# Gathered graph messages with a layer norm: the ramp-down of a software pipeline over the last groups is spread from 12 groups to 36, and the last node block is written out

## The chip, the cores and the metric

The kernel runs on one core of a Trainium2 chip. The metric is the device time of one execution in microseconds (us), as a median over runs. A core has a matrix engine (TensorE, PE in the profile), a vector engine (VectorE, DVE), a scalar engine (ScalarE, ACT), GpSimd (POOL), a queue engine (SyncE, SP) that here only issues transfers, and 16 DMA engines that they share.

## The reference, cut to what matters

There are 12,500 nodes with 64 features (`x`) and 200,000 edges, sorted by their target `dst`; `src` is random. Targets are drawn as 12,500·u² with u uniform, so low nodes have most edges; towards the end of the list a group of 512 edges moves on by some 64 nodes.

```python
def ssp(x): return softplus(x) - log(2.0)
nodes = x[stack([src, dst], 1)].reshape(E, 128)              # gather both ends of each edge
gates = (ssp(edge_state @ We1 + be1) @ We2 + be2) * (1 - sigmoid(5 * (edges_distance - 3.5)))
h = ssp(nodes @ Wn1 + bn1) @ Wn2 + bn2
message_sum = zeros_like(x).at[dst].add(h * gates)           # scatter-add into the targets
new_state = x + (ssp(message_sum @ Ws1 + bs1) @ Ws2 + bs2)   # a small network on every node
out = layernorm(x + new_state)                               # over the 64 features, no scale or shift
```

## The kernel before, in words

The edges are cut into NG = 391 groups of 512, numbered 0 to 390 (`last`). The last group is partly padding: it has three gathers, not four. A group goes through these operations, each a small function:

- `gather` (L176): GpSimd issues four indirect transfers of 128 rows of `x` each into `xg`. In every 32nd group, the last of them 388, the fourth set of rows comes by single-row transfers on SyncE (L191) in place of the fourth gather. `load` brings edge features (`eT`, L197) and a 42-row window of a prepared table (`wns`, L204) on SyncE.
- `onehot` (L209, VectorE) writes a one-hot code of each edge's target within the window beside the gathered rows.
- `transposes` (L217, four on TensorE) into the PSUM tile `tx`, `xcopy` (L222, ScalarE) out of it.
- `layer1`: edge part (L226 bias, L228), node part (L233, four matmuls), into the PSUM tile `z`.
- `exps` and `logs` (L243, L246, ScalarE), then `softplus` (L251, VectorE).
- `layer2`: bias and edge part (L257, L260), node part (L265, eight matmuls), into `gh`.
- `hcut` and `message` (L270, L274, VectorE).
- `scatter` (L278, four matmuls) sums messages into the window, and `window` (L287, two adds on VectorE at an offset read from a table) adds the result into `sums`, the running message sum of all nodes in SBUF.

The main loop has steps i. Every engine runs its instructions in the order in which the loop writes them; waits between engines are put in by the framework from what is read and written, and an add at an offset known only at run time counts as touching all of `sums`. The pipeline is staggered: step i transposes group i+3, does layer 1 of group i+1, layer 2 of i-1 and the scatter of i-3. There are two `tx` buffers, which the transposes, the late scatters and the node blocks share, two of `z` and two of `gh`.

At step `both` = `last` - CATCH_UP = 378 this stagger is reduced at one go: two groups get layer 2 in that step, three are scattered in the next, and from then on step i transposes i+2, does layer 1 of i+1, layer 2 of i and the scatter of i-1 (into `tx`, no longer into a corner of `z`). The last group is written into the last steps by hand, its softplus in an edge and a node part.

The nodes are cut into blocks of 512 (the first has 212, the last two 256). `block_steps` gives the number of groups after which a block's sums are surely complete; towards the end 359, 368, 376, 384, 388 and 391. `node_block` then queues five parts in `todo`, and a step takes one of them: `hidden` (L306, matmuls that read `sums`) with `clamp` (L312 loads `x`, L314 and L315 on VectorE); `logs` and `ssp` (L318, L319 ScalarE, L322 VectorE); `layer2` of the block (L327, L330) with `center` (L334 to L337: add, mean over features, subtract); `square` and `variance` (L341 ScalarE, L345 and L346 VectorE); `root` and `store` (L350, L351 ScalarE, L356 to L359 VectorE, and L360, the store on SyncE). Parts that are left after the loop run one behind the other.

Of the kernel before, what the change touches and what calls it, by code (L numbers as in the profile page):

```python
# [40 lines left out]
F32 = mybir.dt.float32  # L42
BF16 = mybir.dt.bfloat16
I32 = mybir.dt.int32
AF = mybir.ActivationFunctionType
# [19 lines left out]
CATCH_UP = 12  # L65
# [7 lines left out]
def node_blocks(N):  # L73

    rest = N - NB
    first = rest % NB
    assert rest > 0 and first % 2 == 0 and first <= HE
    sizes = ([first] if first else []) + [NB] * (rest // NB) + [HE, HE]
    return [(sum(sizes[:i]), n) for i, n in enumerate(sizes)]
# [18 lines left out]
def gnn_resnorm_kernel(ctx: ExitStack, tc: tile.TileContext, a: dict, out: bass.AP, E: int):  # L98
# [52 lines left out]
    half = const.tile([P, 1], F32, name="half")  # L151
    ones3 = const.tile([PIECES, HE], BF16, name="ones3")
# [78 lines left out]
    def layer1_node(g, h):  # L231
        zn = zs[g][:, h, HE * (1 - h) : HE * (2 - h)]
        nc.tensor.matmul(zn, wns[:, g % REST, h, :], xTs[g][:, h], start=True, stop=True, skip_group_check=True)  # L233
# [29 lines left out]
    def layer2_node(g, h):  # L263
        for t in range(2):
            nc.tensor.matmul(ghs[g][:, 1, 2 * t + h, :], ss[g][:, 1 + h, t, :], wn2, start=False,  # L265
                             stop=h == 1 and t == 1, skip_group_check=True)
# [14 lines left out]

    def window(g):
        for h in range(2):
            base = nc.values_load(base_i[0:1, 2 * g + h : 2 * g + h + 1], engines=[DVE], min_val=0, max_val=N - 1,
                                  skip_runtime_bounds_check_because="it was clamped to these bounds")
            part = sums[h * D : (h + 1) * D, bass.ds(base, W)]
            nc.vector.tensor_add(part, part, scs[g][h * D : (h + 1) * D, h * W : (h + 1) * W])  # L287

    def node_block(first, n, pool):
# [20 lines left out]
        def clamp():  # L310
            t["y"] = tile3("y")
            nc.sync.dma_start(t["y"], x[rows, :].rearrange("(q p k) d -> p q k d", q=nq, k=2))  # L312
            t["l"], t["zb"] = (pool.tile([P, HE], F32, name=name, bufs=2) for name in ("l_s", "zb"))
            nc.vector.tensor_scalar(t["l"], t["z"], packed["bs1"], BIG, OP.add, OP.min)  # L314
            nc.vector.tensor_scalar(t["zb"], t["z"], packed["bs1"], None, OP.add)  # L315
# [17 lines left out]
        def center():  # L333
            nc.vector.scalar_tensor_tensor(t["y"], t["y"], 2.0, t["u"][:, :nq], OP.mult, OP.add)  # L334
            mean = small("mean")
            nc.vector.tensor_reduce(mean, t["y"], AX.X, OP.add)
            nc.vector.scalar_tensor_tensor(t["y"], mean.to_broadcast([p, nq, 2, D]), -1.0 / D, t["y"], OP.mult, OP.add)  # L337
# [5 lines left out]
        def variance():  # L343
            t["v"] = small("var")
            nc.vector.tensor_reduce(t["v"], t["y2"], AX.X, OP.add)  # L345
            nc.vector.tensor_scalar(t["v"], t["v"], 1.0 / D, EPS, OP.mult, OP.add)  # L346

        def root():
            t["r"] = small("rstd")
            nc.scalar.activation(t["r"], t["v"], AF.Ln)  # L350
            nc.scalar.activation(t["r"], t["r"], AF.Exp, scale=-0.5)  # L351

        def store():

            v, r = t["v"], t["r"]
            nc.vector.tensor_mul(v, v, r)  # L356
            nc.vector.scalar_tensor_tensor(v, v, -0.5, r, OP.mult, OP.mult)
            nc.vector.scalar_tensor_tensor(r, v, 1.5, r, OP.add, OP.mult)
            nc.vector.tensor_mul(t["y"], t["y"], r.to_broadcast([p, nq, 2, D]))  # L359
            nc.sync.dma_start(out[rows, :].rearrange("(q p k) d -> p q k d", q=nq, k=2), t["y"])  # L360

        def then(f, g):
            def both():
# [4 lines left out]
        return [(hidden, clamp), (None, then(logs, ssp)), (layer2, center), (None, then(square, variance)),  # L368
                (None, then(root, store))]
# [6 lines left out]
    with tc.manual_schedule():  # L376
# [4 lines left out]
        with tc.tile_pool(name="prep", bufs=1) as prep:  # L381
# [23 lines left out]
            nc.vector.memset(half, 0.5)  # L405
            nc.vector.memset(ones3, 1.0)
# [40 lines left out]
            nc.vector.tensor_add(brow[:, 1:3, :], brow[:, 1:3, :], ps[:1, : 2 * D].rearrange("o (i d) -> o i d", d=D))  # L447
            pieces = prep.tile([1, PIECES, 4 * D], BF16, name="pieces")
# [43 lines left out]
        with tc.tile_pool(name="finish", bufs=1) as finish:  # L492
            blocks = list(zip(node_blocks(N), block_steps(N, NG)))
            last = NG - 1
            both = last - CATCH_UP
            second, third, ahead = {}, {}, {}
            for i in range(-3, NG + 1):
                groups = [i - 1] if i < both else [i - 1, i] if i == both else [i]
                second[i] = [g for g in groups if 0 <= g < NG]
                groups = [i - 3] if i <= both else [i - 3, i - 2, i - 1] if i == both + 1 else [i - 1]  # L500
                third[i] = [g for g in groups if g >= 0]
                groups = [i + 3] if i < both else [] if i == both else [i + 2]
                ahead[i] = [g for g in groups if g < NG]
            todo, complete = [], 0
# [9 lines left out]
            for i in range(-3, NG + 1):  # L514
                part = todo.pop(0) if todo else None
                at(load, i + LOADS)
                fetch(i)
                if i > 0:
                    at(gather, i + AHEAD - 1)
                if i < both:  # L520
                    if 0 <= i + 1:
                        zs[i + 1] = z_tile()
                    for g in third[i]:
                        scatter(g, zs[i + 1][:, 1, HE : HE + 2 * W])
                    for g in second[i]:
                        layer2_edge(g)
                elif i + 1 < last:
                    zs[i + 1] = z_tile()
                if i + 1 < last:
                    at(layer1_edge, i + 1)  # L530
                    at(layer1_node, i + 1, 0)
                    at(layer1_node, i + 1, 1)
                if part and part[0] and i + 2 < last:
                    part[0](tx_tile())
                for g in ahead[i]:
                    transposes(g)
                if i + 1 < last:
                    at(exps, i + 1)
                    if i < both:
                        at(logs, i + 1)  # L540
                for g in ahead[i]:
                    xcopy(g)
                if i >= both and i + 1 < last:
                    logs(i + 1)
                if i + 2 == last:
                    zs[last] = z_tile()
                    layer1_edge(last)
                for g in second[i]:
                    if i >= both:
                        layer2_edge(g)  # L550
                    if i + 2 == last:
                        layer1_node(last, 0)
                        layer1_node(last, 1)
                    layer2_node(g, 0)
                    layer2_node(g, 1)
                if i + 2 == last:
                    for some in (edge, node):
                        exps(last, some)
                        logs(last, some)
                if i + 1 < last:  # L560
                    at(softplus, i + 1)
                if i >= both:
                    for g in third[i][:-1]:
                        scatter(g, tx_tile()[:, : 2 * W])
                        window(g)
                    for g in third[i][-1:]:
                        scatter(g, tx_tile()[:, : 2 * W])
                    for g in second[i]:
                        hcut(g)
                        message(g)  # L570
                for g in third[i][-1:]:
                    window(g)
                    complete = g + 1
                if i < both:
                    for g in second[i]:
                        hcut(g)
                        message(g)
                for g in ahead[i]:
                    at(onehot, g + 2)
                if i + 2 == last:  # L580
                    softplus(last, edge)
                    softplus(last, node)
                if part:
                    if i + 2 < last:
                        part[1]()
                    else:
                        node_part(part)
                while blocks and blocks[0][1] <= complete and i < last:
                    todo += node_block(*blocks.pop(0)[0], finish)
            for parts in zip_longest(todo, *[node_block(*block, finish) for block, step in blocks]):  # L590
                for part in parts:
                    if part:
                        node_part(part)
# [147 lines left out]
```

## Time and profile before

| | |
|---|---|
| median of 9 runs | 1997.34 us (1994.05 to 2012.62) |
| the profiled execution: its time, its span | 1993.79 us, 1992.0 us |
| mean granted TensorE clock | 0.981 |
| TensorE busy | 1885.7 us, 95% |
| GpSimd busy | 1474.4 us, 74% (1551 gathers of 950 ns) |
| VectorE, ScalarE busy | 1050.3 us (53%), 919.2 us (46%) |
| start of the last gather on GpSimd | 1950.58 us |
| start of the last group's transposes | 1963.87 us |

The page's busy time is an average over stages with different limits, so it is read together with the chain of waits (who released whom, followed back from the end), the timeline (instructions in order of time) and busy times by stretches of the span. In these views a line such as `PE z L233 x4` is four matmuls of line 233 into the tile `z`; an entry in square brackets is the idle time in front of an instruction and who ended it. The mean duration of a pipelined matmul is longer than its share of the engine's time; the chain shows the shares.

### The profile page before, as it was taken

To read this page: it belongs to the slowest core of one execution; us is meant where nothing else is said; L and a number is where in the kernel's file an instruction comes from. 1 tells how busy PE (TensorE), PEld (TensorE's weight loads), DVE (VectorE), ACT (ScalarE), POOL (GpSimd) and SP (SyncE) were. 2 spreads that over 40 slices of the span, in tenths; PEclk is the share of its full clock that TensorE was granted. 3 is DMA by queue.
4 is the path that set the end of the run, shared out by engine and by line. 5 is a ranking of instruction groups with operands and counts; after the bars stand their busy time and mean duration, and the time that the engine had idled before them with its cause. 6 is when DMAs were issued, how large, how long until landed. Compare 5 with 4: busy or idle time off the path is not lost.

```text
span 1992.0 us, 42101 instructions
## 1 busy us (share of the span) xinstructions
PE 1885.7 (95%) x11378; PEld 1514.5 (76%) x11378; DVE 1050.3 (53%) x2752; ACT 919.2 (46%) x1322; POOL 1474.4 (74%) x1555
## 2 busy tenths in 40 slices
PE   4999999999999999999999999999999999999996
PEld 4888888888777777777777778777777788777775
DVE  4455555555544545545545545555555555555555
ACT  1355455544444444444444445444444445444443
POOL 7777777777777777777777777777777777777771
PEclk9999999999999989999999989999999989999998
DMA  8422222222222222222222222222222222222221
GB/s 231 141 67 67 69 67 71 66 67 70 62 72 67 58 69 69 59 69 62 66 67 66 69 62 64 70 70 68 64 66 68 68 63 71 69 68 71 71 62 28
DMA packets 171021, 143.15 MB, mean 72 GB/s; under 512 B 46507, under 2 KB 142947, under 8 KB 170778
## 3 DMA queue, kind: packets, MB, share of 16 engines
q1 hardware_dynamic: 119778, 87.95, 15.3%
q0 software_dynamic: 49632, 50.92, 11.6%
q10 hardware_dynamic: 1368, 1.51, 0.4%
q8 instruction: 95, 1.56, 0.3%
q14 instruction: 148, 1.21, 0.2%
HBM read 130.57 MB, written 9.63 MB: 70 GB/s over the span
## 4 chain that ended last, share of the span: by engine, by line
PE 58%; DMA 23%; POOL 8%; issue 5%; DVE 2%; ACT 2%; DVEq 1%; POOLq 0%; ACTq 0%
DMA xg<-in_x,src_i 22%; PE gh L265 11%; PE z L233 10%; PE gh L260 8%; POOL xg L176 8%; PE z L228 8%; PE tx L217 6%; PE z L278 6%; PE gh L257 4%; PE z L226 3%; PE z L471 2%; ACT u L246 1%; DMA wns<-in_Wn 1%; ACT u L243 1%; PE tx L330 1%
## 5 line engine op out<-in xcount | busy, mean ns | idle before, releaser
L176 POOL DMA_INDIRECT xg<-in_x,src_i x1551 | 1474.2, 950 | 476.9 <-issue 305.5
L251 DVE SCALAR_TENSOR_TENSOR s<-u,z 128x768 f32<-128x768 f32 x392 | 373.2, 952 | 838.7 <-ACT u L246 766.4
L243 ACT ACTIVATE u<-z 128x768 f32<-128x768 f32 x392 | 317.4, 810 | 970.0 <-PE z L233 970.0
L233 PE MATMUL z<-xT,wns 106*128 106x256 f32 x1564 | 413.1, 387 | 0.0
L265 PE MATMUL gh<-consts,s 128*128 128x64 f32 x3128 | 396.4, 270 | 0.0
L265 PEld LDWEIGHTS gh<-consts,s 128*128 128x128 f32 x3128 | 392.9, 196 | 0.1
L246 ACT ACTIVATE u<-u,one 128x768 f32<-128x768 f32 x392 | 366.0, 934 | 12.4
L233 PEld LDWEIGHTS z<-xT,wns 106*128 106x128 f32 x1564 | 303.7, 194 | 45.4 <-issue 0.5
L217 PE MATMUL tx<-consts,xg 128*106 128x128 f32 x1552 | 277.3, 283 | 59.7 <-DMA xg<-in_x,src_i 53.9
L217 PEld LDWEIGHTS tx<-consts,xg 128*106 128x106 f32 x1552 | 195.0, 133 | 147.3 <-DMA xg<-in_x,src_i 97.5
L260 PE MATMUL gh<-consts,s 128*128 128x128 f32 x1564 | 280.9, 302 | 0.0
L228 PE MATMUL z<-eT,consts 128*128 128x256 f32 x782 | 280.0, 440 | 0.0
L260 PEld LDWEIGHTS gh<-consts,s 128*128 128x128 f32 x1564 | 205.7, 191 | 89.4 <-issue 88.7
L278 PE MATMUL z<-xg,msg 128*128 128x84 f32 x1500 | 236.3, 280 | 0.0
L222 ACT COPY xT<-tx 106x512 f32<-106x512 f32 x391 | 221.7, 567 | 10.0 <-PE tx L217 9.8
L278 PEld LDWEIGHTS z<-xg,msg 128*128 128x128 f32 x1500 | 199.0, 193 | 0.0
L270 DVE TENSOR_TENSOR h<-gh,cut 128x256 f32<-128x256 f32 x391 | 166.0, 425 | 13.7 <-PE gh L265 1.3
L274 DVE TENSOR_TENSOR msg<-gh,h 128x256 f32<-128x256 f32 x391 | 166.0, 425 | 13.5
L228 PEld LDWEIGHTS z<-eT,consts 128*128 128x128 f32 x782 | 118.8, 191 | 48.0 <-issue 2.2
L257 PE MATMUL gh<-row,ones 3*128 3x512 bf16 x391 | 151.3, 387 | 0.0
L287 DVE TENSOR_TENSOR sums<-sums,z 64x42 f32 x750 | 144.3, 192 | 13.0 <-issue 6.1
L209 DVE TENSOR_TENSOR xg<-consts,rel 128x168 f32<-128x168 f32 x391 | 126.8, 325 | 1.1 <-issue 0.4
(79 smaller groups left out, 590.8 us busy)
## 6 DMA issues: line engine op xcount, KB each, us to landing
eT<-in_eT SPq DMA_DIRECT2D x391, 128.0 KB
xg<-in_x,src_i POOLq DMA_INDIRECT x1551
xr<-in_x SPq DMA_DIRECT2D x1536, 0.2 KB
wns<-table SPq DMA_DIRECT2D x782, 21.0 KB
table<-tb SPq DMA_DIRECT2D x14, 448.0 KB
sums<-in_xT SPq DMA_DIRECT2D x7, 455.0 KB
y<-in_x SPq DMA_DIRECT2D x23, 128.0 KB
out<-y SPq DMA_DIRECT2D x23, 128.0 KB
```

Of the source, the lines that this page charges most:

```text
L176: nc.gpsimd.indirect_dma_start(out=xg[:, k, :D], out_offset=None, in_=x, in_offset=bass.IndirectOffsetOnAxis(ap=src_i[:, g, k : k + 1], ax ...
L217: nc.tensor.transpose(tx[:, k, :], row, ident)
L222: nc.scalar.copy(xT, xTs[g])
L228: nc.tensor.matmul(zs[g][:, 0, :HE], we1.rearrange("a h d -> a (h d)"), eTs[g], start=False, stop=True, skip_group_check=True)
L233: nc.tensor.matmul(zn, wns[:, g % REST, h, :], xTs[g][:, h], start=True, stop=True, skip_group_check=True)
L243: nc.scalar.activation(us[g][:, part], z_of(g)[:, part], AF.Exp)
L246: nc.scalar.activation(us[g][:, part], us[g][:, part], AF.Ln, bias=one)
L251: nc.vector.scalar_tensor_tensor(ss[g].rearrange("p i t e -> p (i t e)")[:, part], us[g][:, part], BIG, z_of(g)[:, part], OP.min, OP.max)
L257: nc.tensor.matmul(gh, ones3[:, :P], row3.rearrange("q i k d -> q (i k d)"), start=True, stop=False, skip_group_check=True)
L260: nc.tensor.matmul(v[:, 0, t], ss[g][:, 0, t, :], we2, start=False, stop=False, skip_group_check=True)
L265: nc.tensor.matmul(ghs[g][:, 1, 2 * t + h, :], ss[g][:, 1 + h, t, :], wn2, start=False, stop=h == 1 and t == 1, skip_group_check=True)
L278: nc.tensor.matmul(sc, msgs[g][:, 2 * t : 2 * t + 2, :].rearrange("p h f -> p (h f)"), xgs[g][:, 2 * t : 2 * t + 2, D:DW], start=t == 0, s ...
```

## The change

The ramp-down begins earlier and is spread. With `ends` = 390 - 30 = 360: an extra scatter at step 354, no transposes at steps 360 and 362, an extra layer 2 at 366 and an extra scatter at 372. Before step 360 the order on TensorE is scatter, whole layer 2, layer 1, transposes; from 360 on a step's order is transposes and copy of group i+1, layer 1 of i+1, layer 2 of i with `hcut` and `message`, softplus of i+1, scatter and window of i-1 (of i-2 up to step 371), then the node block's matmuls. The loop ends at step 388, and the last group's work is written out behind it.

The node blocks are 212 and then 512 throughout, so the last is one of 512, complete at 391. A block now has eight parts. `fetch` (the load of `x`) and `center` (subtract the mean of `x`) run four and two groups before the block is complete. The mean over features of the second weight and bias is subtracted from these once, in the preparation, so that the sum of both comes out centered. Six parts remain: `hidden` with `clamp`; `logs` with `ssp`; `layer2` with `add`; `square` with `variance`; `root` with `scale`; `store`, now one step later, and on ScalarE's queue for all blocks but the last. In the last steps (i > 382) a step takes a second part if that has no matmuls, which concerns block 384: steps 385 to 387 take two parts each. The two offsets of a window are loaded together.

```diff
-CATCH_UP = 12
+CATCH_UP = 30
...
-    sizes = ([first] if first else []) + [NB] * (rest // NB) + [HE, HE]
+    sizes = ([first] if first else []) + [NB] * (N // NB)
...
+    def window_bases(g):
+        _, window_at[g] = nc.values_load_multi_w_load_instructions(
+            base_i[0:1, 2 * g : 2 * g + 2], engines=[DVE], min_val=0, max_val=N - 1,
...
-        def center():
+        def add():
             nc.vector.scalar_tensor_tensor(t["y"], t["y"], 2.0, t["u"][:, :nq], OP.mult, OP.add)
-            mean = small("mean")
-            nc.vector.tensor_reduce(mean, t["y"], AX.X, OP.add)
-            nc.vector.scalar_tensor_tensor(t["y"], mean.to_broadcast([p, nq, 2, D]), -1.0 / D, t["y"], OP.mult, OP.add)
...
+        def store():
+            queue = nc.sync if first + n == N else nc.scalar
+            queue.dma_start(out[rows, :].rearrange("(q p k) d -> p q k d", q=nq, k=2), t["y"])
...
-        return [(hidden, clamp), (None, then(logs, ssp)), (layer2, center), (None, then(square, variance)),
-                (None, then(root, store))]
+        return [(None, fetch), (None, center), (hidden, clamp), (None, then(logs, ssp)), (layer2, add),
+                (None, then(square, variance)), (None, then(root, scale)), (None, store)]
...
+            mean = prep.tile([P, 3], F32, name="mean_w")
+            nc.vector.tensor_reduce(mean[:, :2], ws2, AX.X, OP.add)
+            nc.vector.tensor_reduce(mean[:1, 2:], brow[:, 3, :], AX.X, OP.add)
+            nc.vector.scalar_tensor_tensor(ws2, mean[:, :2].to_broadcast([P, 2, D]), -1.0 / D, ws2, OP.mult, OP.add)
...
-            both = last - CATCH_UP
+            ends = last - CATCH_UP
...
+            for i in range(-3, NG):
+                groups = [i - 1] if i < ends + 6 else [i - 1, i] if i == ends + 6 else [i]
+                second[i] = [g for g in groups if g >= 0]
+                groups = ([i - 3] if i < ends - 6 else [i - 3, i - 2] if i == ends - 6 else [i - 2]
+                          if i < ends + 12 else [i - 2, i - 1] if i == ends + 12 else [i - 1])
                 third[i] = [g for g in groups if g >= 0]
+                ahead[i] = [i + 3] if i < ends else [i + 2] if i == ends + 1 else [i + 1] if i > ends + 2 else []
...
+            for i in range(-3, last - 1):
+                parts = [todo.pop(0)] if todo else []
+                if i > last - 8 and todo and not todo[0][0]:
+                    parts.append(todo.pop(0))
...
+                else:
+                    for g in ahead[i]:
+                        transposes(g)
+                        xcopy(g)
+                    layer1(i + 1)
+                    exps(i + 1)
+                    logs(i + 1)
                     for g in second[i]:
+                        layer2(g)
                         hcut(g)
                         message(g)
+                    softplus(i + 1)
+                    for g in third[i]:
+                        scatter(g, tx_tile()[:, : 2 * W])
+                        window(g)
+                    for f in hidden:
+                        f(tx_tile())
                 for g in ahead[i]:
                     at(onehot, g + 2)
+                for _, f in parts:
+                    f()
...
+            zs[last] = z_tile()
+            transposes(last)
+            xcopy(last)
+            layer1(last)
+            for some in (edge, node):
+                exps(last, some)
+                logs(last, some)
+            for g in range(last - 2, last + 1):
+                window_bases(g)
+            layer2(last - 1)
+            scatter(last - 2, tx_tile()[:, : 2 * W])
+            softplus(last, edge)
+            hcut(last - 1)
+            message(last - 1)
+            layer2_edge(last)
+            scatter(last - 1, tx_tile()[:, : 2 * W])
+            softplus(last, node)
+            window(last - 2)
+            layer2_node(last)
+            window(last - 1)
+            hcut(last)
+            message(last)
+            scatter(last, tx_tile()[:, : 2 * W])
+            window(last)
+            for part in centered:
+                node_part(part)
```

## The prediction

> **What bounds the kernel now.** I read the page's busy times first, then the chain of waits, the timeline of the last 180 us, and the waits of the queues.
>
> The chain between 1900 and 1946 us (start, length, what) shows two regimes:
>
> ```profile
> 1901.88 0.95 POOL xg L176
> 1903.13 2.37 DMA xg<-in_x,src_i
> 1905.55 0.32 PE tx L217
> ...
> 1936.55 0.63 PE z L228 x2
> 1937.18 0.86 PE z L233 x4
> 1938.04 0.44 PE tx L217 x4
> 1938.48 0.32 PE gh L257
> 1938.80 0.64 PE gh L260 x4
> 1939.44 0.84 PE gh L265 x8
> 1940.28 0.46 PE tx L278 x4
> 1940.95 0.63 PE z L228 x2
> ```
>
> Up to 1905 us the last of a group's four transposes waits for its gather: GpSimd issues one gather after another, each 1.25 us after the one before (0.95 busy, 0.30 issue), 4.99 us for a group, and its rows can be used 3.67 us after the issue began (1901.88 to 1905.55). After that TensorE sets the pace, 4.41 us for a group: layer 1 0.21+0.63+0.86 = 1.70, transposes 0.44, layer 2 0.32+0.64+0.84 = 1.80, scatter 0.46. So TensorE, 95% busy on the page, has only 0.58 us a group to spare, and GpSimd, 74% busy, is the clock.
>
> The timeline shows where this ends:
>
> ```profile
> 1820.25 0.32 PE L217 MATMUL tx<-consts,xg 128*106 128x128 f32 x1 [0.57 <-DMA xg<-in_x,src_i]
> ...
> 1950.58 0.94 POOL L176 DMA_INDIRECT xg<-in_x,src_i  x1 [0.30 <-issue]
> ...
> 1963.87 0.62 PE L217 MATMUL tx<-consts,xg 128*106 128x128 f32 x4 [0.22 <-PE z L233]
> ...
> 1975.65 0.20 DVE L287 TENSOR_TENSOR sums<-sums,tx 64x42 f32 x1 [0.43 <-issue]
> ...
> 1976.00 0.67 PE L306 MATMUL tx<-sums,consts 128*128 128x256 f32 x2 [3.02 <-DVE sums L287]
> ```
>
> Group 390 could be transposed at 1950.58 + 3.67 = 1954.25, but is at 1963.87: TensorE is 9.6 us late. From there to the end of the span it takes another 28.1 us. The change can only touch these two numbers: GpSimd's gathers are not altered, they run without a pause, and until step 360 TensorE waits for them. The last line is for later: the 256-node block complete after group 387 waits for the add of group 389's window, which was written just ahead of it. Block matmuls wait for every window add written before them, needed or not.
>
> **The change part by part.**
>
> *Nothing, up to step 360.* The new order of layer 2 in the step, the joint load of two offsets, the block's `center` moved ahead (0.84 us in every eighth group on VectorE), and about 1 us of new VectorE work in the preparation (two reductions and two small operations, 0.2 to 0.4 us each by the rows of L435 and L453) all lie under GpSimd; VectorE there waits 8.34 us for a transfer (L461). Without that cover it would be 1 us. Centering's two operations (0.42 each) leave the tail.
>
> *TensorE's work from there.* Transposes of group 363 still wait for their gather at 1820.25 and end at 1820.57 (step 361). From then to the transposes of 390 TensorE has layer 1 of 28 groups (47.6), layer 2 of 29 (52.2), 29 scatters (13.3), 26 transposes (11.4), and four blocks of 0.86 + 0.8 (6.6): 131.2 us. Without one stall it would be there at 1951.8, just ahead of the gather's 1954.25. So the ramp fits exactly, and each stall after 1820 counts in full.
>
> *Stalls.* Take a late step with t = 0 at its transposes. Layer 1's node part starts at 1.28 (the copy arrives at 1.27: 0.60 + 0.59 and two hand-overs) and ends at 2.15, layer 2 at 3.95, the scatter at 4.41. VectorE starts hcut at 4.15, message at 4.60, softplus at 5.05 (0.95), and only then the window, which ends at 6.40. Before, the window that a block matmul needed came from the step ahead of it.
> - `hidden` now follows this window: it could start at 4.41 and starts at 6.40, plus 0.25 because a block that waited takes 1.13 and not 0.86 (1947.29 in the chain). Four blocks (steps 361, 370, 377, 385): 9.0 us.
> - After a block's `layer2` both `tx` buffers are taken until the window is added: the next transposes wait 1.2 and lose 0.2 more, at steps 363 and 379: 2.8. At 372, with two scatters, `layer2` itself waits 1.5 + 0.3: 1.8.
> - Paired parts of block 384. ScalarE's queue gets Exp behind `clamp` on VectorE, and the next copy behind both: layer 1 of 387 waits 1.15. Square waits for `add`: the transposes of 388 wait 1.25 (buffer) and layer 1 0.7. The store on ScalarE waits in step 387 for `scale`, which ends after hcut, message, softplus, window, onehot and five operations, 3.4 us after ScalarE got there; the next copy is behind it, so layer 1 of 389 waits 3.6 with the restart. Together 6.7.
>
> Sum 20.3: transposes of 390 at 1820.57 + 131.2 + 20.3 = 1972.1, or 8.2 us later than before.
>
> The price of the waiting store is taken from SyncE's row (us in total, times, longest):
>
> ```profile
> SPq L360 <- DVE y L359: 213.5, 26, 24.9
> ```
>
> A store that is not ready holds its queue for up to 24.9 us; there only prefetched loads stood behind it. I take ScalarE's queue to hold likewise. Single stores at steps 366, 375 and 382 find `scale` done 0.5 us before and cost an issue of some 0.42 under ScalarE's idle time. Bounds: 0 if the queue passes a waiting store, 3.6 if not. [...]
>
> *The tail from the transposes of 390.* Layer 1 has its result at 2.34; four Exp/Ln pieces take 2.17 as at 1967.18; VectorE does hcut and message of 389 to 5.3, softplus to 6.0; layer 2's node part to 6.9; hcut and message of 390 to 7.95, scatter to 8.6, window to 9.05. Then the block alone: hidden 1.05, clamp 0.5, Exp and Ln 1.0, ssp 0.45, layer2 1.24 (at half clock as at 1978.92), add, square and variance 1.33, two roots 0.46, three small operations 0.6, scale 0.42: 16.1. From the last VectorE operation to the end it takes 4.55 in the trace (1987.46 to 1992.0), and I add 0.3 for a store twice as large: 21.0, against 28.1 now, a gain of 7.1. One block of 512 costs what one of 256 did, give or take 0.15 per operation.
>
> **Sum.** 1972.1 + 21.0 = 1993.1, or 1.1 us longer than the span of 1992.0. The profiled execution took 1993.79, 3.55 less than the median, so the median goes from 1997.34 to 1998.4. A measurement of this kernel can tell about 0.3%, 6 us, from no change.
>
> **The rivals.**
>
> *Faster.* The stalls are hidden, because the adds finish earlier than I have them, or the blocks do not wait for the step's own window. With half the stalls the transposes of 390 come at 1962 and the median is 1988.3; with none TensorE meets the last gather at 1954.25, the span is 1975.3 and the median 1980.6. For it: the work sum meets the gather within 2.5 us. Against it: the wait at 1976.00, and VectorE's order in a late step.
>
> *Slower, by TensorE's clock.* Two windows, with busy times and, behind them, the granted clock, DMA share and GB/s:
>
> ```profile
> 1905.00:1920.00 15.00, 13.05 (x84) 10.41 (x82) 6.88 (x18) 6.12 (x8) 11.34 (x13) 1.00 0.30 80
> 1978.00:1992.00 14.00, 3.62 (x11) 2.38 (x11) 5.86 (x23) 2.42 (x9) 0.00 (x0) 0.50 0.06 15
> ```
>
> Three gaps of some 0.9 us between 1917 and 1920 left the clock at 1.00; after the gap of 3.02 before 1976.00 it is 0.50. The store's gap at step 388 is 3.6 us long, and behind it 10.2 us of matmuls lead to the last scatter. At half clock for a third of them the cost is 3.4, for all of them 10.2: median 2001.8 to 2008.6, some 2005. It decides from a gap of about 3 us. [...] Since the clock also falls in mid-run (0.86 from 700 to 750 us with TensorE busy for 48.69 of 50), idle time is not its only cause, and a stretch of 150 us that TensorE bounds, in place of 60, meets such a drop more often.
>
> *The stores do nothing.* SyncE's 213.5 us of waiting were off the path, as loads run five groups ahead; then only the wait on ScalarE is new. This is in the forecast.
>
> **How the numbers follow.** No change within 6 us (1992 to 2003) 0.47: stalls between 13 and 25 us. Faster 0.26, at 1981 to 1990. Slower 0.27, at 2004 to 2009. A tenth is left out at each end: 1986 to 2007.
>
> **What would show it.** Right: a gather wait at the transposes of 363 and none of weight after it; those of 390 at 1970 to 1975; `hidden` in steps 361, 370, 377 and 385 released by the window add after about 2 us; layer 1 of 389 released by a ScalarE copy that stands behind a store; 21 us from there to the end. Wrong: transposes still waiting for gathers after 1900, those of 390 before 1962, or a last part of under 18 us or over 24.

## The result and the profile after

The change made the kernel slower: 2059.9 us median of ten runs against 1996.3 of 31 runs of the kernel before, a ratio of 1.029 [1.026, 1.031]. The forecast was 1998.4 with 2007.0 as the upper end. The profiled execution took 2076.4 us (span 2074.6) and is one of the slower ones, at a mean granted clock of 0.932 where the nine fast runs have 0.942 to 0.968 and the profiled execution of the kernel before 0.981, so its sizes are somewhat too large.

The page of the kernel after, busy time and the clock in 40 slices:

```profile
PE 1936.3 (93%) x11373; PEld 1576.6 (76%) x11373; DVE 1048.5 (51%) x2745; ACT 922.9 (44%) x1317; POOL 1470.6 (71%) x1555
...
PEclk9999999999989989999999999899999999859686
```

GpSimd's work is the same and ends no later (1946.7 us against 1951.5), so the loss is not there. The clock has changed: the clock records of the two traces, 18 before and 40 after, hold full and half clock only, so by the mean clock TensorE ran at half speed for 2 x 0.068 x 2074.6 = 282 us, against 2 x 0.019 x 1992.0 = 76 us before. The starts of the groups' Exp (L243 before, L246 after) say where it counts. Those of groups 353 and 360, first before and then after:

```profile
1780.68 0.81 ACT L243 ACTIVATE u<-z 128x768 f32<-128x768 f32 x1 [2.78 <-PE z L233]
1814.65 0.81 ACT L243 ACTIVATE u<-z 128x768 f32<-128x768 f32 x1 [1.81 <-PE z L233]
```

```profile
1782.24 0.81 ACT L246 ACTIVATE u<-z 128x768 f32<-128x768 f32 x1 [2.10 <-PE z L235]
1863.03 0.81 ACT L246 ACTIVATE u<-z 128x768 f32<-128x768 f32 x1 [9.06 <-PE z L235]
```

At group 353 the kernel after is 1.6 us behind the one before, which is nothing; at 359 it is 41.0 behind, at 360 48.4, at 380 71.0, at 389 77.9. All drops of the clock before 1780 us were made up again, since TensorE waits for gathers there (28.8 us of idle time in front of its transposes from 93 to 1780 us; 49.1 in the kernel before). **So the whole loss lies behind step 352, and three fifths of it is there by group 360.**

The chain of waits from 1793 us on (start, length, what), in the stretch where the chain of before was gathers and dense matmuls:

```profile
1793.67 0.05 issue
1793.86 1.46 DMA xr<-in_x
1795.32 0.09 issue
1795.40 0.43 PE tx L217
...
1808.36 0.43 DVE msg L282
1808.83 0.89 PE z L286 x4
1809.73 0.54 PE gh L260
1810.26 1.15 PE gh L263 x4
1811.42 1.60 PE gh L269 x8
1813.02 0.32 PE z L226
1813.34 1.15 PE z L228 x2
1814.49 1.72 PE z L235 x4
1816.23 0.82 ACT u L246
1817.08 0.94 ACT u L249
1818.05 0.54 DVE s L254
...
1819.33 0.43 DVE h L278
1819.79 0.43 DVE msg L282
1820.26 1.15 PE z L286 x4
```

Two things stand here. The transposes of group 356 wait for single rows (`xr`) that SyncE issued too late. And then one step is a closed ring: scatter (L286), layer 2, layer 1, Exp, Ln, softplus, window, hcut, message, scatter; 11.4 us from one scatter to the next (1808.83 to 1820.26, at half clock) in place of 4.99. Nothing in it waits for a gather.

SyncE's waits, after (us in total, times, longest):

```profile
SPq L191 <- DMA out<-y: 166.9, 13, 21.6
SPq L204 <- DMA out<-y: 56.3, 6, 18.4
```

Before, SyncE waited 213.5 us for `y` to be ready and 0.9 us for a store to land. Now it issues no store but the last, and waits 223.2 us for stores to land. The trace shows why. Every transfer of SyncE and ScalarE in it names one of eight semaphores, on which its landing is recorded. From 90 us on SyncE's transfers take the eight in one order, 2685 times the next one and 24 times the next but one; the 24 left out are those that ScalarE's 24 stores take, in the same order. 23 of these stores take one that SyncE uses again, and SyncE's next transfer on it starts after the store each time, 1.84 to 5.61 us after its issue (median 2.00). One such place, in the timeline (start, duration, engine, line):

```profile
1767.37 0.36 SPq L197 DMA_DIRECT2D eT<-in_eT  x1
1776.77 0.88 SPq L204 DMA_DIRECT2D wns<-table  x2
```

SyncE stands still for 9.0 us between the two; ScalarE issued its store of a block in between, at 1774.79, on the semaphore that the second line uses next.

The predicted store on a computing engine, timeline of ScalarE and TensorE:

```profile
2039.28 0.38 ACTq L382 DMA_DIRECT2D out<-y  x1
2039.70 0.58 ACT L222 COPY xT<-tx 106x512 f32<-106x512 f32 x1 [3.67 <-DVE y L378]
2040.34 1.21 PE L235 MATMUL z<-xT,wns 106*128 106x256 f32 x4 [3.01 <-ACT xT L222]
```

This is the wait of layer 1 of group 389 that the prediction named, 3.01 us long. The windows that answer to those of before (PE, PEld, DVE, ACT, POOL busy, clock, DMA share, GB/s), and the last group's transposes:

```profile
1905.00:1920.00 15.00, 15.00 (x99) 11.57 (x99) 7.86 (x21) 8.36 (x11) 11.34 (x13) 1.00 0.32 81
2045.00:2074.00 29.00, 17.78 (x62) 13.40 (x61) 9.75 (x29) 4.52 (x10) 0.00 (x0) 0.50 0.03 8
```

```profile
2045.52 1.06 PE L217 MATMUL tx<-consts,xg 128*106 128x128 f32 x4
```

From 1905 to 1920 TensorE has no idle time left, as meant; but the tail behind 2045.52 runs at half clock throughout and takes 29.0 us, not less than the 28.1 of before.

### The profile page after: what moved, and what is told of

Its sections match the earlier page's. It is cut to its first block, busy times and chain, and to the rows that moved or that the text cites. A ratio compares the mean times of both kernels' runs of the same rounds, so it can differ in the third digit from the quotient of the medians.

```text
span 2074.6 us, 41732 instructions
## 1 busy us (share of the span) xinstructions
PE 1936.3 (93%) x11373; PEld 1576.6 (76%) x11373; DVE 1048.5 (51%) x2745; ACT 922.9 (44%) x1317; POOL 1470.6 (71%) x1555
## 4 chain that ended last, share of the span: by engine, by line
PE 72%; DMA 11%; POOL 5%; issue 4%; DVE 4%; ACT 3%; SPq 1%; DVEq 0%; POOLq 0%; ACTq 0%
PE gh L269 13%; PE z L235 13%; PE gh L263 10%; PE z L228 10%; DMA xg<-in_x,src_i 9%; PE tx L217 7%; PE z L286 6%; POOL xg L176 5%; PE gh L260 5%; PE z L226 3%; PE z L501 2%; PE tx L321 1%; ACT u L249 1%; ACT u L246 1%; DVE s L254 1%
## 5 line engine op out<-in xcount | busy, mean ns | idle before, releaser
L246 ACT ACTIVATE u<-z 128x768 f32<-128x768 f32 x392 | 316.9, 808 | 970.5 <-PE z L235 970.4
L235 PE MATMUL z<-xT,wns 106*128 106x256 f32 x1564 | 431.9, 400 | 4.0 <-ACT xT L222 4.0
L269 PE MATMUL gh<-consts,s 128*128 128x64 f32 x3128 | 413.7, 278 | 0.0
L269 PEld LDWEIGHTS gh<-consts,s 128*128 128x128 f32 x3128 | 403.3, 202 | 0.0
L235 PEld LDWEIGHTS z<-xT,wns 106*128 106x128 f32 x1564 | 313.8, 202 | 58.1 <-ACT xT L222 8.7
L217 PE MATMUL tx<-consts,xg 128*106 128x128 f32 x1552 | 263.1, 286 | 34.8 <-DMA xg<-in_x,src_i 28.8
L263 PE MATMUL gh<-consts,s 128*128 128x128 f32 x1564 | 291.2, 311 | 0.0
L228 PE MATMUL z<-eT,consts 128*128 128x256 f32 x782 | 290.5, 455 | 0.0
L263 PEld LDWEIGHTS gh<-consts,s 128*128 128x128 f32 x1564 | 214.1, 199 | 93.9 <-issue 92.1
L286 PE MATMUL z<-xg,msg 128*128 128x84 f32 x1432 | 215.9, 275 | 25.5 <-DVE msg L282 25.5
L286 PEld LDWEIGHTS z<-xg,msg 128*128 128x128 f32 x1432 | 196.8, 199 | 28.5 <-issue 14.4
L260 PE MATMUL gh<-row,ones 3*128 3x512 bf16 x391 | 156.0, 399 | 0.0
L302 DVE TENSOR_TENSOR sums<-sums,z 64x42 f32 x716 | 137.9, 193 | 8.4 <-issue 1.6
```

Source lines behind the costliest of these rows:

```text
L217: nc.tensor.transpose(tx[:, k, :], row, ident)
L228: nc.tensor.matmul(zs[g][:, 0, :HE], we1.rearrange("a h d -> a (h d)"), eTs[g], start=False, stop=True, skip_group_check=True)
L246: nc.scalar.activation(us[g][:, part], z_of(g)[:, part], AF.Exp)
L260: nc.tensor.matmul(gh, ones3[:, :P], row3.rearrange("q i k d -> q (i k d)"), start=True, stop=False, skip_group_check=True)
L263: nc.tensor.matmul(v[:, 0, t], ss[g][:, 0, t, :], we2, start=False, stop=False, skip_group_check=True)
L286: nc.tensor.matmul(sc, msgs[g][:, 2 * t : 2 * t + 2, :].rearrange("p h f -> p (h f)"), xgs[g][:, 2 * t : 2 * t + 2, D:DW], start=t == 0, s ...
```

## The experiments

**Stores or ramp.** Theory A (queue) blames the late loads of SyncE, theory R (ramp) the ring that the extra scatter at step 354 closes. The first two edits:

```diff
 # stores back
-            queue = nc.sync if first + n == N else nc.scalar
-            queue.dma_start(out[rows, :]...
+            nc.sync.dma_start(out[rows, :]...
 # scatter at 360
-                groups = ([i - 3] if i < ends - 6 else [i - 3, i - 2] if i == ends - 6 else [i - 2]
+                groups = ([i - 3] if i < ends else [i - 3, i - 2] if i == ends else [i - 2]
...
```

e1: 

> The changed kernel with all stores back on SyncE; all else as changed (1996.3 us before, 2059.9 us after). Theory A (queue): the loss begins with SyncE, which waits for stores of ScalarE to land before it may issue its own transfers (223 us of such waits), so that its loads come late, the single rows of group 356 last of all (TensorE waits 8.5 us), and TensorE's clock halves behind that. By A alone the waits of SyncE for out<-y are gone, the wait at xr is gone, and the time is 1990 to 2005. Theory R (ramp): from step 354 the scatter of group i-2 waits in step i for a message that VectorE computes in step i-1 behind the softplus of that step; scatter, layer 2, layer 1, Exp, Ln, softplus, window, hcut and message then follow one another, 0.5 + 1.8 + 1.7 + 1.8 + 0.95 + 0.4 + 0.9 and four hand-overs of 0.2 = 8.9 us a step against 5.0, for six steps: 23 us at full clock and 40 at half clock. By R the time stays at 2020 to 2045.

e2: 

> The changed kernel with the extra scatter at step 360 in place of 354 (scatters stay at i-3 up to 359); stores stay on ScalarE. Theory R: the loop of steps 354 to 359 is gone, 23 to 40 us less; what is left is the wait for the rows of group 356 and the clock behind it: 2005 to 2035. Theory A: SyncE is as late as before, the wait at xr of some 8 us and the half clock behind it stay: 2045 to 2065.

e3: 

> Both edits: stores on SyncE, extra scatter at step 360. If A and R are all of it, the time is what was predicted for the change, 1990 to 2003. If over 2010, something else costs: the late order from step 360, where window adds and block matmuls follow one another, or the tail.

e4 (the kernel before, with the two lines of `store` as changed): 

> The kernel before with one edit: stores (but the last block's) on ScalarE's queue. Theory A: SyncE waits for landings of stores, its lead over TensorE falls from some 20 us to 10 or less, and where the rows of a group by rows come late TensorE waits and its clock halves: 2000 to 2025, with waits SPq <- DMA out<-y of 100 us or more. Theory R: without the new ramp the same late loads cost nothing, since TensorE makes up for them in the groups that wait for gathers: 1994 to 2000.

These four ran on a chip that granted TensorE a mean clock of 0.82 to the kernel before too (2581.6 us), so that TensorE set the pace all along (an estimated 6.6 us a group, from this time and 391 groups, against 4.99 for the gathers): ratios 1.044 [1.037, 1.051], 1.048 [1.041, 1.055], 1.029 [1.023, 1.036] and 1.011 [1.003, 1.018]. No expected time can be read against that. One thing can: from Exp of group 353 to that of 362, e1 took 94.3 us, e2 65.2, e3 61.7, e4 58.7. With the stores on SyncE in both, e1 and e3 differ in the scatter alone: the ring costs some 30 us there too. The same kernels were run again:

e5: 

> Again the changed kernel with all stores back on SyncE, since the chip of the first four runs granted TensorE a mean clock of only 0.82 for the kernel before too, so that TensorE and not GpSimd set the pace all along. There the stretch from group 353 to 362 took 94 us with the scatter at 354 and 62 with it at 360. On a chip that grants the full clock, theory A (queue) expects 1990 to 2005, theory R (ramp loop) 2015 to 2045, with 8.9 us a group or more from 354 to 360 and no wait at xr.

e6: 

> Again both edits, stores on SyncE and the extra scatter at step 360. If queue and ramp loop are all of it, 1990 to 2003 at full clock; above 2010 something else costs.

e7: 

> Again the changed kernel with the extra scatter at 360 and its stores on ScalarE, for a chip that grants the full clock. It differs from the run with both edits (1.010 of before) in the queue of the stores alone. Theory A (queue): SyncE waits for landings (150 us or more), its lead falls under 10 us, TensorE waits for the rows of group 356 and its clock halves: 2030 to 2050. If the ramp loop was all, 2015 to 2025, as with both edits.

e8: 

> Again the kernel before with its stores on ScalarE and nothing else. Theory A: the lead of SyncE falls as in the changed kernel and a late row costs a wait and a stretch of half clock, of which what falls ahead of the last 60 us is made up again under GpSimd's gathers: 1997 to 2015. If stores on ScalarE were harmless by themselves: 1993 to 2000.

Full clock again. e5: 2052.9 us (four runs, 2036.7 to 2077.9), 1.024 [1.016, 1.033]: SyncE waits for `y` as it did before (195.4 us), no wait for `xr`, and still most of the loss; groups 353 to 359 take 63.3 us, 10.6 each, against 29.6 before. This is R, a little above its range, and refutes A as the main cause. e7: 2027.6, 1.014 [1.010, 1.018], between its two expectations: the ring is gone and with it 1.5%, the waits for `xr` (8.9 us, 6.0 of them at group 356) and for landings (217.4 us) are not. e6 (four runs): 2019.7, 1.010 [1.004, 1.016]. That is 0.4% less than e7, which the intervals do not tell apart, and 17 us above what was hoped for both edits, so there is a third cause. e8: 1.0025 [0.9993, 1.0057]: by itself, on the kernel before, the move of the stores cannot be told from nothing, though SyncE waited 195.9 us for landings there (162.8 at L204, 33.1 at L191).

**The third cause: block matmuls behind the window add.** The timeline and a window (TensorE busy, clock, DMA share, GB/s) of e6:

```profile
1824.20 2.05 PE L321 MATMUL tx<-sums,consts 128*128 128x256 f32 x4 [1.78 <-DVE sums L302]
```

```profile
1825.00:1855.00 30.00, 30.00 (x99) 0.50 0.25 55
```

The predicted gap before `hidden` in step 361 is there with 1.78 us (I had 2.0), and behind it the clock is 0.50 for 30.7 us, although TensorE shows no idle time in it. Another gap, of 1.55 us ahead of the transposes of group 363, lies 6 us before it; a gap of 1.69 us before `hidden` at 1883.58 was followed by no half clock at all. The edit puts `hidden` and `clamp` right behind layer 1, and the block's `layer2` and `add` behind message, ahead of softplus, scatter and window:

```diff
                     layer1(i + 1)
+                    if hidden and hidden[0].__name__ == "hidden":
+                        parts[0][0](tx_tile())
+                        parts[0][1]()
+                        parts, hidden = parts[1:], []
 ...
                         message(g)
+                    if hidden:
+                        parts[0][0](tx_tile())
+                        parts[0][1]()
+                        parts, hidden = parts[1:], []
                     softplus(i + 1)
```

e9 (both edits and this one): 

> Both edits, and in the late order (from step 360) hidden with clamp right behind layer 1, layer2 with add right behind message, both ahead of softplus, scatter and window, so that no block matmul waits for the step's own window add. Theory S: the rest of 1.010 comes from TensorE's gaps of 1.3 to 1.8 us before block matmuls (7.4 us in all) and the half clock that began at the first of them (30.7 us in the run with both edits, which costs half of that where TensorE bounds): gaps under 0.6 us, no half clock from 1815 to 1860, 1980 to 1998. Rival: TensorE runs without slack from step 360 and its clock falls in such a stretch whatever its gaps: 2010 to 2025.

e10 (the same with CATCH_UP = 18): 

> The same with the ramp begun at step 372 in place of 360 (CATCH_UP 18), so that TensorE waits for gathers, with slack to make up for losses, for 60 us longer. By theory S it is the same as the run beside it, within 5 us (1978 to 2000). If the length of the stretch without slack decides, it is 5 to 20 us faster than that run.

e9: **1982.9 us, 0.990 [0.987, 0.993]**, faster than both kernels. All of TensorE's waits for `sums` before the tail are gone. A late stretch of it:

```profile
1840.00:1950.00 110.00, 109.12 (x673) 1.00 0.28 65
```

109.12 of 110 us busy at full clock: this stretch without slack did not lose the clock, and the time is far below the 2010 to 2025 of the rival, which refutes it. Not all of S's expectation held: a gap of 1.64 us was left ahead of the transposes of group 363, with 17.1 us of half clock from 1820 us on. e10: 0.996 [0.993, 0.999], 0.6% slower than e9 where I had expected the same or better; its twelve runs lie between 1983.6 and 2009.7. Why the shorter ramp scatters so was not followed up and stays open.

**Each fault put back by itself.** On e9:

e11 (stores on ScalarE): 

> The fastest kernel so far (stores on SyncE, extra scatter at 360, block matmuls early: 0.990 of before) with one edit, its stores on ScalarE's queue. Theory A (queue): SyncE waits 150 to 220 us for landings, loads for groups 353 to 360 come late, TensorE waits 6 to 9 us there with some half clock behind it: 0.994 to 1.002. If SyncE's lateness costs nothing once the rest is repaired: 0.988 to 0.993.

e12 (scatter at 354): 

> The same fastest kernel with one other edit, the extra scatter at 354. Theory R (ramp loop): groups 353 to 359 take over 8.9 us each, 10 or more at half clock, against 4.9, which is 24 to 36 us lost with no slack behind it to make it up: 1.000 to 1.010. If the loop cost only through the gaps that follow it: 0.990 to 0.996.

e12: 2020.4 us, 1.010 [1.006, 1.013], as R expected; 61.6 us for groups 353 to 359, 10.3 each, and the chain shows the ring and nothing else (Exp at 1806.38, next Exp at 1818.07). e11: 2021.3 us, 1.012 [1.007, 1.016], 2.2% above e9 where A expected 0.4 to 1.2%. So the stores cost 2.2% in the repaired kernel, 0.4 to 0.5% in the changed one (e5, e7 against e6), where the intervals overlap, and nothing that can be told in the kernel before. The faults do not add up; that they hide behind one another because each makes the same TensorE late is likely, but was not tested.

**Why the stores cost 2.2%.** Three candidates: late rows (`xr`), late block loads (`y`), and the store on ScalarE, which in the kernel after held the copy behind it for 3.67 us (at 2039.70).

```diff
 # e13, e15: rows earlier
-    return [g for g in range(P // ROWS + 4, NG - 2, P // ROWS)]
+    return [g for g in range(P // ROWS + 12, NG - 2, P // ROWS)]
 # e14: load of y earlier
-                if blocks and complete >= blocks[0][1] - 4 and not centered:
+                if blocks and complete >= blocks[0][1] - 7 and not centered:
```

e13 (e11 with rows earlier): 

> The repaired kernel with its stores on ScalarE (1.012 of before, against 0.990 with stores on SyncE), and the groups by rows moved by eight (44, 76 and so on to 364; one such group less, so one more gather, 1.25 us). A group's 128 rows are then loaded ten steps before its transposes and not two. If the price of the stores is the wait for late rows (5.5 us at group 356, 8.5 in the changed kernel) and the half clock behind it: 0.992 to 0.999. If it lies elsewhere, in the block loads that VectorE waits for, or in ScalarE's queue: 1.006 to 1.014.

e14 (e11 with `y` earlier): 

> The repaired kernel with its stores on ScalarE, and the block's load of x seven groups ahead of its block and not four, its centering two groups ahead as before. If the price of the stores is VectorE's wait for this load (28 us in nine waits, up to 4.6) and the message behind it: 0.992 to 0.999. If it is the late rows: 1.006 to 1.014.

e15 (e9 with rows earlier): 

> The control: groups by rows moved by eight with the stores on SyncE. No row is late there, so it differs from the repaired kernel (0.990) by the extra gather and by group 388, now four gathers: 0.989 to 0.993.

e13: 0.998 [0.994, 1.001]; e14: 1.002 [0.999, 1.005]; e15: 0.989 [0.985, 0.993], so the move of the rows alone changes nothing that can be told (e9: 0.990). Late rows are 1.4% of the 2.2. In e11, TensorE's timeline has:

```profile
1790.08 0.43 PE L217 MATMUL tx<-consts,xr 128*106 128x128 f32 x1 [5.48 <-DMA xr<-in_x]
```

In e13 no such wait is left, though SyncE still waits 171.4 us for landings (91.0 at L191, 80.4 at L204). e14 gained 1.0% on e11, between its two expectations. VectorE's waits for `y` (28.6 us in e11) are gone there, but waits for rows (9.1 us) remain, and the two profiled executions differ by 0.9 us only, so where this gain lies is not shown. e13 still stands 0.9% above e15, which differs in the stores alone. In e13:

```profile
1955.77 0.59 ACT L222 COPY xT<-tx 106x512 f32<-106x512 f32 x1 [3.67 <-DVE y L378]
1956.40 2.08 PE L235 MATMUL z<-xT,wns 106*128 106x256 f32 x4 [3.01 <-ACT xT L222]
```

The store holds ScalarE, TensorE idles 3.01 us, and the matmuls behind that take some 1.8 times as long as those of the step before: layer 1's node part 2.08 us in place of 1.13, layer 2's 1.81 in place of 1.00. From group 363 to 388 every Exp starts 1.1 us earlier in e13 than in e15, that of group 389, behind this store, 3.0 us later. The last group's transposes come 4.9 us later, and from them to the end of the span e13 takes 29.5 us, e15 23.5: all of the 10.8 us between the two spans lies behind the store, although VectorE's waits for `y` (24.7 us) remain in e13 too.

## Why the prediction was wrong, point by point

The sign was open in the prediction (0.26, 0.47, 0.27) and the time lay 53 us above the upper end.

- **"Nothing, up to step 360": the step that failed.** The description of the change lists an extra scatter at step 354, but the prediction's list of what happens up to step 360 has no term for it: it was put at nothing without a reason. Up to step 359 message of group i-1 stands behind softplus of i+1 on VectorE, and layer 1 of i+1 behind the scatter on TensorE. With the scatter of i-2 in step i these two orders close a ring that no gather is in: from the rows that I had, 0.46 + 1.80 + 1.70 on TensorE, 0.81 + 0.94 on ScalarE, 0.95 + 0.4 + 0.9 on VectorE, and hand-overs, an estimated 8.9 us a step at full clock against 4.99. Measured, mostly at half clock (a mean of 0.64 from 1780 to 1860 us in e12), were 10.3 us a step in e12 and turns of 11.7 us, from Exp to Exp, in the kernel after. The work sum started from the transposes of 363, ending at 1820.57, with a wait for their gather; they came at 1867.67 without one, and those of 390 at 2045.52 in place of 1972.1. Alone the scatter costs 2.0% (e12 against e9).
- **The stalls: right in place and size, wrong in what follows.** `hidden` waited 1.69 to 1.78 us idle (predicted 2.0), the transposes after the block's `layer2` 0.86 (1.2 to 1.4), layer 1 of 389 behind the store 3.01 (3.6). I priced them at 20.3 us as idle time. Removing the block waits (in e6 6.9 us before `hidden`, 1.3 before the block's `layer2`, 1.7 before transposes) brought 2.0% (e6 to e9, 36.8 us of the medians). In the two profiled executions it is 21.4 us of span (2006.1 to 1984.7), with some 27.5 us less of half clock from 1780 us on.
- **The rival of the clock: right in kind, wrong in point and place.** It was to decide "from a gap of about 3 us", at one place. In e6 half clock followed a gap of 1.78 us at step 361, in the kernel after one of 1.26 at 1935 us, for 37.5 us. The gaps of 0.9 us between 1917 and 1920 that were to show short gaps harmless are two in the trace, not three. At the store it came true: a half-clock tail of 29.0 us in the kernel after, against 22.0 in e9 where no store holds. The forecast left half clock behind the store's 3.6 us out, and no run shows a gap of that length without it: it followed all 34 gaps of over 2.0 us that are counted in the last section.
- **"The stores do nothing": failed.** It took SyncE's 213.5 us of waiting for granted as off the path, and that they would fall away. They became 223.2 us of another wait, for stores to land; the rows of group 356 were late by 8.5 us. I looked at what queues behind ScalarE's store on ScalarE, not at who else waits for it.
- **The tail: nearly right without a hold.** 21.0 us predicted, 22.0 (e9, at a clock of 0.92 from 1940 to 1980 us) to 23.7 (e5) with stores on SyncE, 28.1 before. In the changed kernel it took 29.0, above the 24 that the prediction named as a sign of being wrong.
- **The rival "faster" gave the right number for the repaired kernel, in part by luck.** With no stalls it had 1980.6; e9 took 1982.9 and e15 1981.9. But it has TensorE meet the last gather at 1954.25. In the profiled executions the transposes of 390 come at 1962.73 (e9) and 1957.56 (e15), against 1963.87 before, so 11.6 and 4.0 us after the last gather would let them (9.6 before). Of e9's 7.3 us of span 6.2 come from the shorter tail and only 1.1 from the ramp; its 17.1 us of half clock from 1820 us on cost an estimated 8.5, and e15, without half clock there, has 6.3 from the ramp.
- **What the change is worth.** The idea brings 1%; three orders in it cost 3.9% (1.029 to 0.990): scatter at 354, stores, block matmuls, which brought 1.5, 0.4 (not clear of the noise) and 2.0% when they were repaired one behind the other (e7, e6, e9).

## What to carry to other kernels

When an instruction is moved to an earlier step, write down what it waits for on each engine's own order and follow it round once: if the path comes back to the same instruction one step later, its length is a floor for the step, whatever the busy times say. A gap on a TensorE that sets the pace cost more here than its own length: 30.7 us of half clock came behind 1.78 us in e6, 37.5 behind 1.26 in the kernel after, so it is priced with what the clock does behind it. A store that was moved to another queue still bound the first here: SyncE, whose transfers name the same eight semaphores, waited 223.2 us for ScalarE's stores to land. Look for waits of the kind "load <- store" in the queue's own waits.

## What the runs showed of the hardware

How short a gap can be that half clock follows was not expected. Counted are the gaps in which neither matmul nor weight load runs and which begin at full clock, in the traces of before, after and e5 to e15 without their first 85 and last 45 us, and how many of them have half clock begin in the gap or within 3.5 us behind it:

| gap, us | gaps | followed by half clock |
|---|---|---|
| 0.3 to 0.6 | 1113 | 15 (1%) |
| 0.6 to 0.9 | 196 | 15 (8%) |
| 0.9 to 1.2 | 67 | 24 (36%) |
| 1.2 to 2.0 | 43 | 21 (49%) |
| over 2.0 | 34 | 34 |

The 107 half-clock stretches that began in these 23.3 ms of full clock would fall behind an estimated 2% of moments picked at random, so the first row is no more than chance. What decides whether a gap of 1 to 2 us is followed by half clock, and how long it then lasts, is not shown.

In these traces each of the 111 half-clock stretches that the span's end did not cut lasted a multiple of 3.4 us (3.4 in 47 of them, then 6.8, 10.2, 13.7, 17.1, 20.5, 30.7 and more, up to 58.0), also while TensorE showed no idle time (30.00 of 30.00 us busy from 1825 to 1855 in e6). At half clock layer 1's node part took 1.72 us in the chain (after, 1814.49) in place of 0.86 (before, 1937.18).
